# Moving the query, key and value projection of a graph layer from the sort stage to the gather stage

## The chip, the core and the metric

The kernel runs on one core of a Trainium2 chip. A core has five engines with a queue of instructions each: PE (TensorE, matrix multiplications; its weight loads are listed as PEld), DVE (VectorE), ACT (ScalarE), POOL (GpSimd) and SP (SyncE, which issues DMAs). The engines work side by side and wait for each other through semaphores; each engine takes its own instructions strictly in order. The metric is the device time of one execution in microseconds (us). Inputs are read from device memory and the result is written there within that time.

## The reference, cut to what matters

A graph layer for 6250 nodes with 256 features and 206,250 edges (src, dst). Three parts are added up: attention over the edges of the graph, linear attention over all nodes, and a mixture of eight experts.

```python
xn = layernorm(x)
# 1. graph attention: h = xn @ W (64 columns, 4 heads)
e = exp(leaky_relu(el[src] + er[dst], 0.2));  w = e / segment_sum(e, src)[src]
gnn = elu(segment_sum(w * h[dst], src) + b)            # per head, 4 x 64 = 256
# 2. linear attention, 4 heads of 32
q, k, v = split(rmsnorm(xn, g_pre) @ w_qkv)            # 128 columns each
k = softmax([mem_k, k], over the nodes);  q = softmax(q, over 32) * 32 ** -0.5
context = k @ [mem_v, v]                               # 32 x 32 a head
mix = rmsnorm((context . q) @ w_out + b_out, g_out) + xn
x = x + gnn + mix
# 3. experts: x = x + tokens + sum over the 2 best of 8 of weight * (gelu(tokens @ w1 + b1) @ w2 + b2)
```

For the linear attention every node has to contribute to `context` before any node's output can be computed, and the softmax of the keys needs a maximum over all nodes (or one that is corrected as it grows).

## The kernel before, in words

The nodes are cut into 49 tiles of 128, and `groups` are 13 runs of up to four tiles. The work goes through two stages.

**Sort stage.** The edges arrive in no order that helps. They are spread over 1612 columns of 128 and sorted into 25 pairs of node tiles by matrix products with one-hot matrices: `sort_batch` (L370 to L464) takes 32 columns at a time, in 51 batches. A batch compares on DVE (`ob`, L387), counts on PE (`n_ps`, L395), scans on DVE (`inc`, L399), ranks with two products on PE (`r_ps`, L419 and L420), takes a maximum on DVE (`rank`, L427), builds a 128 x 4096 one-hot on DVE (`ohp`, L448) and places the edges with 32 matmuls on PE (`g_ps`, L454). The loop at L526 runs `project` (L303) for a group and then three batches; the last twelve batches follow without a projection (L545). `project` loads a group of x on SP, normalizes it on ACT (`xn`, L338), transposes it on PE (`tp`, L343), and multiplies it with `wcat` (L348), a weight matrix of 456 columns: 384 for queries, keys and values, 72 for the table of the graph attention. ACT copies queries into `q_all` (L351), keys and values into `kv` (L352) and the rest into `tab` (L355), scaling the first two with `rn`, which DVE makes in small steps (L325 to L328). The table goes to device memory.

`context` (L467) is a generator: each `next` gives one step of instructions. It begins with one maximum over all keys on DVE (L468); then, step by step beside the last sort batches, POOL subtracts the maximum from the keys of a group (L498), ACT takes exponentials (L499) and PE adds keys times values to one accumulator (L502). Its last step makes the 128 x 256 matrix `cw`, which holds context and output weights.

**Gather stage.** `pack(q)` (L875) turns pair q of node tiles into gather addresses: DVE compares and scans, and seven rounds of DVE one-hots (`ohc` L923, `rc` L930, `ohp` L935) and 16 PE matmuls each (`s_ps`, L940) place the edges. Its last step issues the gathers of both tiles on POOL: 35 indirect DMAs a tile (L972) into `xe`, of which there are three buffers. So the gather of tile b + 3 can begin when tile b has been summed and its `xe` is free. For a tile, `look` (L980) makes logits (PE transposes, the ACT copy `ohT` at L1001, PE products at L1009), `weights` (L1016) turns them into edge weights on DVE and ACT, and four calls of `sums` (L1035) build weighted one-hots on DVE (`ohw`, L1041) and multiply them with the gathered rows on PE (`a_ps`, L1048). ACT's copy `a_s` (L1106) ends the tile.

Between these the loop at L1085 places other work. After each of the four `sums` of a tile it runs steps of later packs (up to `b * S + k + 3` steps of the list `packs`, eight steps a pack), and then `some_more` (L1058), which takes steps off the list `todo` until a cost is used up: in blocks of four tiles at most FC = 2 a call, 16 calls a block. `todo` begins with `attention()` (L574), 39 steps of cost 2: for each group, a softmax of the queries (L583 to L588), four transposes, products with `cw` and sums of squares (L594 to L601), and an output step that loads x again and stores `base_y` (L612 to L620). When it is used up, the expert weights are loaded (`open_experts`), and after each block the 22 steps of its experts (`finish_steps`) join the list: hidden layers (L775, L783) and results (L791, L795). Two packs, 0 and 1, are made ahead of the first tile (L1075 to L1080).

A helper `later` (L567) makes an instruction follow pack 0 in its engine's order without a wait. The order of each engine's queue is otherwise set by the framework's scheduler from the order of the program and its priorities. PSUM, in which PE writes, is divided into pools; in the gather stage `yps` has two buffers and `hps` one.

Of the kernel before, what the change touches and what calls it, by code (L numbers as in the profile page):

```python
# [1 line left out]

# [33 lines left out]
def tile_gps_layer(  # L36
# [53 lines left out]
    KW = 2 * HID + 1  # L90
    O_TAB = 3 * HID
    O_EL = O_TAB + H + FO
    PW = O_EL + H
    assert NPAD > N and PW <= 512 and last > 0
# [141 lines left out]
    with tc.tile_pool(name="ids", bufs=1) as lp:  # L236
# [21 lines left out]
    nc.scalar.dma_start(out=wcat[:, :, :3 * HID], in_=w_qkv.rearrange("(c p) f -> p c f", p=P))  # L258
    nc.scalar.dma_start(
        out=wcat[:, :, O_TAB + H:O_EL], in_=gnn_W.rearrange("(c p) f -> p c f", p=P)  # L260
    )
# [3 lines left out]
    gpre = kp.tile([P, DC], F32, name="gpre")  # L265
# [5 lines left out]
    wo = kp.tile([P, D], F32, name="wo")  # L271
    nc.scalar.dma_start(out=wo, in_=w_out)
    mk = kp.tile([P, NM], F32, name="mk")
    nc.scalar.dma_start(out=mk, in_=mem_kv[0].rearrange("h d m -> (h d) m"))
    mv = kp.tile([P, NM], F32, name="mv")
# [6 lines left out]
    for c in range(DC):  # L282
        wt_ps = mps.tile([FO, P], F32, name="tp")
        nc.tensor.transpose(wt_ps, wcat[:, c, O_TAB + H:O_EL], ident)
# [4 lines left out]
        nc.scalar.copy(wcat[:, c, O_TAB:O_TAB + H], wlr_ps[:, :H])  # L289
        nc.scalar.copy(wcat[:, c, O_EL:PW], wlr_ps[:, H:])  # L290
        nc.vector.tensor_scalar(
            wcat[:, c, :3 * HID], wcat[:, c, :3 * HID], gpre[:, c:c + 1], None, op0=OP.mult
        )

    q_all = qp.tile([P, NT, HID], F32, name="q_all")
    kv = kp.tile([P, NT, KW], F32, name="kv")
    nc.gpsimd.memset(kv[:, :, KW - 1:KW], 1.0)
    kmax = kp.tile([P, HID], F32, name="kmax")
# [4 lines left out]
    def project(t0, n):  # L303
# [10 lines left out]
        for j in range(n):  # L314
# [8 lines left out]
        rn = qw.tile([P, GT], F32, name="rn")  # L323
        nc.scalar.activation(rn[:, :n], var, AF.Sqrt, scale=float(D))
        nc.vector.tensor_mul(rn[:, :n], rn[:, :n], rs)  # L325
        nc.vector.tensor_scalar_max(rn[:, :n], rn[:, :n], 1e-12)
        nc.vector.reciprocal(rn[:, :n], rn[:, :n])
        nc.vector.tensor_scalar_mul(rn[:, :n], rn[:, :n], float(D) ** 0.5)  # L328
        shift = qw.tile([P, GT], F32, name="shift")
        nc.vector.scalar_tensor_tensor(  # L330
            shift[:, :n], stats[:, t0:t0 + n, 0], -1.0, rs, op0=OP.mult, op1=OP.mult
# [3 lines left out]
        for j in range(n):  # L335
# [3 lines left out]
                xn, xt[:, j, :], AF.Identity, bias=shift[:, j:j + 1], scale=rstd[:, t:t + 1]  # L339
# [7 lines left out]
            for c in range(DC):  # L347
# [3 lines left out]
            nc.scalar.activation(q_all[:, t, :], pr[:, :HID], AF.Copy, scale=rn[:, j:j + 1])  # L351
            nc.scalar.activation(  # L352
                kv[:, t, :2 * HID], pr[:, HID:3 * HID], AF.Copy, scale=rn[:, j:j + 1]
            )
            nc.scalar.copy(tab[:, j, :], pr[:, O_TAB:PW])  # L355
# [110 lines left out]

    def context():  # L467
        nc.vector.tensor_reduce(  # L468
            kmax, kv[:, :NT - 1, :HID].rearrange("p t d -> p d t"), axis=AX.X, op=OP.max
        )  # L470
        nc.vector.tensor_max(kmax[:last], kmax[:last], kv[:last, NT - 1, :HID])
        km_ps = mps.tile([HID, P], F32, name="tp")
        nc.tensor.transpose(km_ps, kmax, ident)
        kcol = kp.tile([P, 2], F32, name="kcol")
        nc.vector.tensor_reduce(kcol[:, 0:1], km_ps, axis=AX.X, op=OP.max)
        nc.vector.tensor_reduce(kcol[:, 1:2], mk, axis=AX.X, op=OP.max)
        kmc = kp.tile([P, 1], F32, name="kmc")
        nc.vector.tensor_max(kmc, kcol[:, 0:1], kcol[:, 1:2])
        kr_ps = mps.tile([P, HID], F32, name="tp")
        nc.tensor.transpose(kr_ps, kmc.to_broadcast([P, P]), ident)  # L480
        krow = kp.tile([P, HID], F32, name="krow")
        nc.vector.tensor_copy(krow, kr_ps)
        nkm = kp.tile([P, 1], F32, name="nkm")
# [61 lines left out]
    while batches:  # L545
        sort_batch(batches.pop(0))
        next(steps, None)
    for _ in steps:
        pass
# [714 lines left out]
```

## Time and profile before

| what | us |
|---|---|
| three runs | 4209.87, 4211.42, 4214.99; median 4211.42 |
| the profiled execution | 4182.5 |
| its span, from the first to the last instruction | 4180.7 |
| busy in the span: PE, PEld, DVE, ACT, POOL | 2268.6, 1663.9, 1919.8, 746.2, 1669.8 |
| sort stage: first matmul of the projection, last sort matmul | 25.0, 411.9 |
| first gather begins, last gather ends | 446.2, 3994.5 |
| first tile ends (`a_s`), last tile ends | 617.3, 4145.3 |
| one tile's 35 gathers, first issue to end of the last | 43.4 to 45.7 |

The profile is of one execution. Its page gives busy time by engine, the span cut into 40 slices with the busy share in tenths and the clock that PE was granted, the chain of work that ended last, and groups of instructions by line: how many, busy time in all, mean length in nanoseconds, and after the bar how long the engine had been idle before them and what ended that. Matmuls of a group overlap, so that their busy time divided by their number is less than their mean length; what follows is worked out with the former. Further views give the busy time of each engine in any stretch of time, and who waited for whom.

### The profile page before, as it was taken

Reading aid. Unit: us, or ns where it says so; the run is one execution under the profiler, and the core shown is the slowest. Engines: PE = TensorE matmul, PEld = TensorE weight load, DVE = VectorE, ACT = ScalarE, POOL = GpSimd, SP = SyncE. Lnnn points to the kernel's source line nnn. Section 1 sums busy time; section 2 is a strip of 40 time slices with the busy share of each in tenths; the row PEclk is TensorE's granted clock in tenths of the full one; section 3 lists DMA queues with packets and bytes.
Section 4 is the critical chain, followed back from the end, with each engine's and each line's share of the span. In section 5 each row is a group of like instructions: output and inputs, shape, how many; then the busy total and the mean of one; then the engine's idle time right before and its main releaser. Section 6 shows DMA issues by size and latency. Waiting matters only on the chain. (4 is left out here: it accounts for less than half of the span.)

```text
span 4180.7 us, 39357 instructions
## 1 busy us (share of the span) xinstructions
PE 2268.6 (54%) x15401; PEld 1663.9 (40%) x15401; DVE 1919.8 (46%) x3941; ACT 746.2 (18%) x1653; POOL 1669.8 (40%) x1774
## 2 busy tenths in 40 slices
PE   7877232435254764644765555455364573554677
PEld 4544232324242543433543433334253352442456
DVE  7787444536352443533442523425343452342423
ACT  5542001212111111111111110111111111110122
POOL 1001545454445344344344344544535335344410
PEclk8875555666666877776877776777676686776778
DMA  1020111111121111011011100101101001011100
GB/s 59 28 29 1 21 28 41 37 41 37 34 74 20 22 19 23 18 24 22 12 29 18 25 17 17 30 17 22 25 12 27 18 19 25 13 25 19 23 12 7
DMA packets 106548, 103.75 MB, mean 25 GB/s; under 512 B 42678, under 2 KB 78740, under 8 KB 106356
## 3 DMA queue, kind: packets, MB, share of 16 engines
q0 software_dynamic: 54720, 60.52, 8.4%
q1 hardware_dynamic: 49940, 39.75, 3.3%
q8 instruction: 123, 2.02, 0.2%
q10 hardware_dynamic: 1696, 0.89, 0.1%
q14 instruction: 69, 0.57, 0.0%
HBM read 86.39 MB, written 14.65 MB: 24 GB/s over the span
## 5 line engine op out<-in xcount | busy, mean ns | idle before, releaser
L972 POOL DMA_INDIRECT xe<-table,dst_x x1710 | 1635.7, 957 | 2011.0 <-PE a_ps L1048 1323.2
L1048 PE MATMUL a_ps<-ohw,xe 128*65 128x128 f32 x4400 | 665.1, 307 | 235.7 <-issue 189.3
L1048 PEld LDWEIGHTS a_ps<-ohw,xe 128*65 128x65 f32 x4400 | 590.8, 159 | 314.4 <-issue 243.1
L775 PE MATMUL h_ps<-tokT,w1s 128*128 128x512 f32 (+3 forms) x896 | 442.8, 610 | 235.1 <-ACT hT L783 205.1
L795 DVE SCALAR_TENSOR_TENSOR x<-y_ps,comb,x 128x256 f32<-128x256 f32 x392 | 187.0, 481 | 782.4 <-remote 479.1
L791 PE MATMUL y_ps<-w2s,hT 128*128 128x256 f32 x1568 | 436.7, 413 | 147.6 <-issue 107.2
L791 PEld LDWEIGHTS y_ps<-w2s,hT 128*128 128x128 f32 x1568 | 315.5, 208 | 273.0 <-issue 177.5
L940 PE MATMUL s_ps<-rc,ohp 128*128 128x144 f16 x2525 | 255.1, 260 | 279.5 <-DVE ohp L935 146.8
L1041 DVE TENSOR_TENSOR ohw<-oh,bank 128x1280 f32<-128x1280 bf16 x196 | 321.5, 1641 | 170.1 <-remote 149.3
L940 PEld LDWEIGHTS <-ohp 128*128 128x128 f16 x2525 | 209.6, 114 | 324.2 <-DVE ohp L935 162.9
L1009 PE MATMUL e_ps<-elw,ohT 128*128 128x48 bf16 x588 | 36.2, 199 | 544.7 <-ACT ohT L1001 477.8
L783 ACT ACTIVATE hT<-h_ps,b1s 128x512 f32<-128x512 f32 (+3 forms) x224 | 140.4, 627 | 1018.4 <-remote 531.0
L775 PEld LDWEIGHTS h_ps<-tokT,w1s 128*128 128x128 f32 x896 | 171.8, 214 | 345.7 <-ACT hT L783 226.0
L1001 ACT COPY ohT<-t_ps 128x768 bf16<-128x768 bf16 x98 | 78.3, 799 | 1130.1 <-remote 842.3
L930 DVE TENSOR_TENSOR rc<-ohc,bank 128x1152 f16<-128x1152 f16 (+1 forms) x350 | 231.2, 687 | 64.8 <-remote 62.2
L1009 PEld LDWEIGHTS <-ohT 128*128 128x128 bf16 x588 | 27.0, 106 | 577.2 <-ACT ohT L1001 505.9
L935 DVE TENSOR_TENSOR ohp<-to,bank 128x2048 f16<-128x2048 f16 (+1 forms) x175 | 193.5, 1105 | 0.0
L763 PE MATMUL y_ps<-b2s,cTs 8*128 8x256 f32 x98 | 49.7, 600 | 192.4 <-ACT cTs L761 118.6
L764 DVE TENSOR_TENSOR x<-x,y_ps 128x256 f32<-128x256 f32 x49 | 20.6, 420 | 269.7 <-remote 164.6
L1018 DVE TENSOR_REDUCE z<-e_ps 128x140 f32<-128x420 f32 (+1 forms) x49 | 28.7, 585 | 244.6 <-PE e_ps L1009 224.1
L923 DVE TENSOR_TENSOR ohc<-to,bank 128x1152 f16<-128x1152 f16 (+1 forms) x175 | 119.6, 683 | 0.3 <-ACT to L911 0.2
L448 DVE TENSOR_TENSOR ohp<-rank,iota_h 128x4096 f16<-128x4096 f16 (+1 forms) x51 | 116.1, 2277 | 6.3 <-ACT rank L439 6.0
(273 smaller groups left out, 2568.0 us busy)
## 6 DMA issues: line engine op xcount, KB each, us to landing
xe<-table,dst_x POOLq DMA_INDIRECT x1710
xt<-in_x_dram SPq DMA_DIRECT2D x24, 512.0 KB
base_y<-xt SPq DMA_DIRECT2D x12, 512.0 KB
yt<-base_y SPq DMA_DIRECT2D x9, 512.0 KB
out_dram<-x SPq DMA_DIRECT2D x9, 512.0 KB
w1s<-in_L_ffn_w_dram SPq DMA_DIRECT2D x8, 256.0 KB
w2s<-in_L_ffn_w_dram SPq DMA_DIRECT2D x8, 256.0 KB
table<-tab SPq DMA_DIRECT2D x12, 138.0 KB
```

Of the source, the lines that this page charges most:

```text
L448: nc.vector.tensor_tensor(pairs(ohp[:, :w]), two(rank2[:, :w], P // 2), row(iota_h, P // 2), op=OP.is_equal)
L775: nc.tensor.matmul(h_ps[:, :w], lhsT=w1s[:, e, c, f * P:(f + 1) * P], rhs=held["tokT"][:, c, :w], start=(c == 0), stop=(c == DC - 1),)
L783: nc.scalar.activation(held[e][:, f, :w], h_ps[:, :w], AF.Gelu, bias=b1s[:, k:k + 1])
L791: nc.tensor.matmul(y_ps, lhsT=held[e][:, f, j * P:(j + 1) * P], rhs=w2s[:, e, f, :], start=(f == 0), stop=(f == FC - 1),)
L795: results.append(nc.vector.scalar_tensor_tensor(x2[:, j, :], y_ps, held["comb"][:, j, e:e + 1], x2[:, j, :], op0=OP.mult, op1=OP.add,))
L923: nc.vector.tensor_tensor(pairs(ohc[:, :m]), twos(to[:, 0, t0:t0 + m], U * CW // 2), iota_2[:, :, :U * CW // 2].to_broadcast([P, m, U * CW ...
L930: nc.vector.tensor_tensor(pairs(rc[:, :m, i, :]), pairs(ohc[:, :m]), twos(edges_q[:, t0:t0 + m, i, :], U * CW // 2), op=OP.mult,)
L935: nc.vector.tensor_tensor(pairs(ohp[:, :m]), twos(to[:, 1, t0:t0 + m], P // 2), iota_2.to_broadcast([P, m, P // 2, 2]), op=OP.is_equal,)
L940: nc.tensor.matmul(flat(s_ps), lhsT=ohp[:, t - t0, :], rhs=flat(rc[:, t - t0]), start=(t == 0), stop=(t == NBT - 1),)
L972: nc.gpsimd.indirect_dma_start(out=xe[:, c, :], out_offset=None, in_=table, in_offset=bass.IndirectOffsetOnAxis(ap=dst_x[:, c:c + 1], axis=0),
L1041: nc.vector.tensor_tensor(ohw[:, :n], oh[:, g0:g1, i, None, :].to_broadcast([P, n, H, SN]), ew_s[:, c0:c0 + n, :, None].to_broadcast([P, n ...
L1048: nc.tensor.matmul(a_ps[:, i].rearrange("f h n -> f (h n)"), lhsT=xe[:, c, H:], rhs=ohw[:, c - c0].rearrange("p h n -> p (h n)"), start=(c ...
```

## The change

- `wcat` has 72 columns instead of 456. `project` makes only the table; it keeps `rn_all` and `shift_all`, the scales of all tiles. The buffer `kv` and the maximum over all keys are gone. The weights of queries, values and keys lie in `wqvk`, loaded by three DMAs on ACT's queue.
- `context` moves into the gather stage. It is a new generator of 41 steps: a set-up, three steps for each group and a last step. A group's first step normalizes x again (loaded again, one group ahead) and transposes it; the second makes the keys of four tiles with two matmuls of 512 columns, a running maximum on DVE, the exponentials with the factor `shrink` by which the sum so far is to be corrected, and queries and values tile by tile; the third transposes the exponentials, multiplies them with the values and adds to `sums_c`.
- `todo` begins with `context` and `attention` one after the other, 80 steps of cost 1 instead of 39 of cost 2: with 2 a call that is two steps a call.
- Packs 0, 1 and 2 are made ahead of the first tile. The list of later packs begins with pack 3, and its steps are let in eight later, so that pack 3 and those after it stand where they stood.
- `o_g` and `sq` in `attention` have one buffer instead of two.

```diff
-    O_TAB = 3 * HID
-    O_EL = O_TAB + H + FO
+    O_EL = H + FO
     PW = O_EL + H
...
+    wqvk = qp.tile([P, DC, 3, HID], F32, name="wqvk")
+    for i, k in enumerate((0, 2, 1)):
+        nc.scalar.dma_start(
+            out=wqvk[:, :, i],
+            in_=w_qkv[:, k * HID:(k + 1) * HID].rearrange("(c p) f -> p c f", p=P),
+        )
...
-            nc.scalar.activation(q_all[:, t, :], pr[:, :HID], AF.Copy, scale=rn[:, j:j + 1])
-            nc.scalar.activation(
-                kv[:, t, :2 * HID], pr[:, HID:3 * HID], AF.Copy, scale=rn[:, j:j + 1]
-            )
-            nc.scalar.copy(tab[:, j, :], pr[:, O_TAB:PW])
+            nc.scalar.copy(tab[:, j, :], pr)
...
-    steps = context()
     while batches:
         sort_batch(batches.pop(0))
-        next(steps, None)
-    for _ in steps:
-        pass
...
+    def context():
...
+        for g, (t0, n) in enumerate(groups):
+            v = vs[g % 2]
+            xnT = qw.tile([P, DC, GT * P], F32, name="xnT", bufs=1)
+            for j in range(n):
+                t = t0 + j
+                xn = xn_of()
+                nc.scalar.activation(
+                    xn, xt[:, j, :], AF.Identity, bias=shift_all[:, t:t + 1],
+                    scale=rn_all[:, t:t + 1],
+                )
+                xT_ps = yps.tile([P, DC, P], F32, name="y_ps")
+                for c in range(DC):
+                    nc.tensor.transpose(xT_ps[:, c, :], xn[:, c * P:(c + 1) * P], ident)
+                nc.scalar.copy(xnT[:, :, j * P:(j + 1) * P], xT_ps)
+            if g + 1 < len(groups):
+                xt = load(g + 1)
+            yield
+            w = (n - 1) * P + rows_of(t0 + n - 1)
+            k_ps = hps.tile([P, GT * P], F32, name="h_ps")
+            for c in range(DC):
+                nc.tensor.matmul(
+                    k_ps[:, :w], lhsT=wqvk[:, c, 2], rhs=xnT[:, c, :w],
+                    start=(c == 0), stop=(c == DC - 1),
+                )
+            here = small("here")
+            nc.vector.tensor_reduce(here, k_ps[:, :w], axis=AX.X, op=OP.max)
+            new = small("most")
+            nc.vector.tensor_max(new, most, here)
+            less = small("less")
+            nc.vector.tensor_scalar_mul(less, new, -1.0)
+            shrink = small("shrink")
+            nc.scalar.activation(shrink, most, AF.Exp, bias=less)
+            most = new
+            ekT = qw.tile([P, GT * P], F32, name="ekT", bufs=1)
+            nc.scalar.activation(ekT[:, :w], k_ps[:, :w], AF.Exp, bias=less)
+            for j in range(n):
+                qv_ps = yps.tile([P, 2, HID], F32, name="y_ps")
+                for c in range(DC):
+                    nc.tensor.matmul(
+                        flat(qv_ps), lhsT=xnT[:, c, j * P:(j + 1) * P],
+                        rhs=flat(wqvk[:, c, :2]), start=(c == 0), stop=(c == DC - 1),
+                    )
+                nc.scalar.copy(q_all[:, t0 + j, :], qv_ps[:, 0])
+                nc.scalar.copy(v[:, j, :HID], qv_ps[:, 1])
+            yield
...
+                nc.tensor.transpose(ek_ps[:r, j, :], ekT[:, j * P:j * P + r], ident)
...
+            nc.scalar.copy(ek[:r, :n], ek_ps[:r, :n])
+            c_ps = yps.tile([P, HID + 1], F32, name="y_ps")
+            for j in range(n):
+                nc.tensor.matmul(
+                    c_ps, lhsT=ek[:r, j, :], rhs=v[:r, j, :], start=(j == 0), stop=(j == n - 1)
+                )
+            nc.vector.scalar_tensor_tensor(
+                sums_c, sums_c, shrink, c_ps, op0=OP.mult, op1=OP.add
+            )
+            yield
...
-    todo = [(attention(), [FC] * (3 * len(groups)))]
+    todo = [(chain(context(), attention()), [1] * (6 * len(groups) + 2))]
...
-    for _ in pack(1):
-        pass
+    for q in (1, 2):
+        for _ in pack(q):
+            pass
 
-    packs = [steps for q in range(2, NQ) for steps in [pack(q)] * (NPB + 1)]
+    packs = [steps for q in range(3, NQ) for steps in [pack(q)] * (NPB + 1)]
...
-                while packed < min(len(packs), b * S + k + 3):
+                while packed < min(len(packs), b * S + k - 5):
```

## The prediction

> **What bounds the kernel now.** I read the page's 40 slices first, then busy time by stretches, then who waits for whom, and last the groups by line.
>
> ```profile
> PE   7877232435254764644765555455364573554677
> DVE  7787444536352443533442523425343452342423
> PEclk8875555666666877776877776777676686776778
> ```
>
> Each slice is 104.5 us. The first three (projection and sort) have both PE and DVE near 80%. From the fifth slice on (the gather stage) both are near half and nothing looks like a bound. So I took each stage apart.
>
> *Sort stage.* The first row below holds six projected groups with their 18 sort batches, the second four batches with no projection beside them.
>
> ```profile
> 111.40:242.20 130.80, 116.05 (x1368) 68.73 (x1368) 101.80 (x164) 78.84 (x306) 1.82 (x12) 0.81 0.11 32
> 373.10:400.80 27.70, 17.31 (x272) 10.82 (x272) 23.92 (x38) 3.48 (x17) 0.00 (x0) 0.50 0.00 1
> ```
>
> The columns are length, then busy PE, PEld, DVE, ACT, POOL, then the granted clock. One group takes 130.8/6 = 21.8 us with PE 19.3 and DVE 17.0. A batch alone takes 27.7/4 = 6.93 us with PE 4.33 and DVE 5.98, at a clock of 0.50 against 0.81. Three batches without any projection thus last 20.8 us, nearly as long as three with it: the wide projection fills PE, but it also stands beside the faster clock.
>
> *Gather stage.* One tile of the first ten (gather 891.5 to 935.9, next gather 959.2), cut into five stretches; then the last stretch of a later tile, which has expert work:
>
> ```profile
> 891.50:901.50 10.00, 7.09 (x59) 5.64 (x58) 6.80 (x16) 3.18 (x12) 7.66 (x8) 1.00 0.13 26
> 901.50:911.50 10.00, 0.00 (x0) 0.00 (x0) 7.62 (x19) 2.00 (x4) 7.73 (x8) 0.60 0.14 30
> 911.50:935.90 24.40, 3.36 (x31) 3.37 (x32) 2.34 (x4) 0.80 (x1) 18.61 (x20) 0.50 0.30 70
> 935.90:943.90 8.00, 4.93 (x23) 3.90 (x22) 0.00 (x0) 2.08 (x2) 0.02 (x1) 0.50 0.13 6
> 943.90:959.20 15.30, 11.81 (x76) 9.75 (x74) 13.55 (x38) 3.25 (x12) 0.00 (x0) 0.87 0.00 1
> ```
>
> ```profile
> 3120.70:3136.80 16.10, 16.10 (x133) 13.92 (x133) 14.46 (x19) 1.69 (x3) 0.00 (x0) 0.95 0.00 1
> ```
>
> While POOL gathers (44 us), PE, DVE and ACT come to a halt after some 10 to 20 us and wake when the gather has landed. The real work is done in what is left. There DVE is 89% busy in the early tile (13.55 of 15.3) and PE 100% in the later one (16.1 of 16.1). The halt shows in the waits of the late tiles as ACT waiting for something the profile cannot name:
>
> ```profile
> ACT ohT L1001 <- remote: 561.5, 21, 45.1
> ACT hT L783 <- remote: 531.0, 18, 44.3
> ```
>
> So PE's half of idle time in the gather stage is not free time. What a tile costs in two phases; counted from 0, tiles 2 to 10 end in the first row (nine) and 11 to 46 in the second (36):
>
> ```profile
> 689.00:1306.00 617.00, 251.74 (x1721) 206.30 (x1720) 303.28 (x641) 101.10 (x224) 307.27 (x315) 0.65 0.18 43
> 1306.00:4034.00 2728.00, 1496.14 (x8668) 1095.78 (x8667) 1109.51 (x2374) 389.20 (x582) 1194.80 (x1255) 0.73 0.11 21
> ```
>
> Per tile: 68.6 us with PE 28.0, DVE 33.7, ACT 11.2; then 75.8 us with PE 41.6, DVE 30.8, ACT 10.8.
>
> **The change, part by part.**
>
> ```profile
> L348 PE MATMUL pr<-wcat,xT 128*128 128x456 f32 x196 | 109.8, 690 | 5.9 <-ACT xT L345 5.9
> L791 PE MATMUL y_ps<-w2s,hT 128*128 128x256 f32 x1568 | 436.7, 413 | 147.6 <-issue 107.2
> L468 DVE TENSOR_REDUCE kmax<-kv 128x128 f32<-128x6144 f32 x1 | 11.0, 11044 | 0.0
> ```
>
> 1. *Projection, 456 columns to 72.* In the six groups L348 takes 52.3 us, 8.7 a group. The nearest narrow f32 row is L712 (8 columns, 35.6/196 = 0.18 us); 16 records of that are 2.9, so PE falls from 19.3 to 13.5. ACT loses L351 and L352 (40.7 us), DVE the four rn steps (7.9 us in 13 groups, 0.6 a group): neither led here. What is late next is DVE or the clock. Lower end: DVE alone, 17.0 - 0.6 = 16.4 us a group, a gain of 5.4 x 13 = 70 us. Upper end: three batches as in the second row, 20.8, plus 2 us where the projection's transposes and matmuls get in the batches' way, 22.8: a loss of 13 us. The cold row is the nearest, for the dense matmuls go; I take 20.6, a gain of 15 us.
>
> The granted clock is 0.81 with the wide matmuls and 0.50 without. The Trainium skill, page "TensorE: Matmul & The Clock Gate", section "Part 1: The HAM clock gate (the "warmup" mystery)", says that half clock is the default and that sustained activity lifts it; by that rule alone the stage stays at 20.8 or more, and without it 16.4 would be the better guess. The rule speaks against this change.
>
> 2. *The rest of the sort.* 16 batches lie between 286.7 and 410.9 us, with the 11.0 us reduction, the POOL subtractions (19.0 us), their exponentials and 98 context matmuls (18.1 us) among them. At 6.93 each they take 110.9: a gain of 13 us, bounds 5 and 25.
>
> 3. *Context moved into the gather stage.* In each group of four tiles: 12 transposes at 0.25 (L707, 24.9/98), 4 key records at 0.49 (L775), 16 query and value records at 0.28 (L791, 436.7/1568), 8 context records at 0.185 (L502): PE 11.0 us, 143 in all; with 0.44 for a 256-column record (L598) 176. ACT: four xn at 0.58, four copies at 0.385, eight at 0.264, exponential and copy at 0.6 each, 0.2: 7.4, so 96 us. DVE 1.4 a group and 5 for the set-up, 23 us. The order of the changed program puts 65, 68, 70, 68 and 52 of the 323 context matmuls ahead of the ends of tiles 0 to 4 and all of attention on the five tiles after; the experts open at the same tile as before, so nothing changes from tile 11 on. A context tile has PE 28.0 - 5.9 (its tenth of attention, L594 and L598, 59.1/10) + 28.6 = 50.7. That is 9 more than a late tile, whose free stretch PE fills, so 75.8 + 9 = 85, and 85 - 68.6 = 16 us more: 82 us for five. The new waits stand in ACT's and PE's queues in order: behind a key exponential that waits for PE and for DVE's maximum stand ohT, ew and a_s, the copies that release the next tile's logits and the next gather. Bounds 40 (half of it runs in the gather's first 20 us, where PE is 35% busy) and 125 (the dearer records, and ACT late).
>
> 4. *Attention at double density.* Two steps a call instead of one. DVE's attention (L583 to L619) is 120 us, 12 a tile over ten tiles, 24 over five. DVE leads there at 89%: 12 x 5 = 60, of which some runs early in the gather: 50, bounds 20 and 60. The DVE relief in the context tiles gives nothing back, since PE leads there.
>
> 5. *Third pair ahead.* The eight steps of one pack move from the first two tiles to before the first. POOL's gathers of that pair wait for buffers as before. Nothing, if they fill the halts of the first three gathers; 34 us (the first pack, 412 to 446) if they delay tile 0, whose end the fourth gather waits for. I take 0.
>
> 6. *SP and POOL queues.* 13 more loads of x (512 KB) on SP, each issued a group ahead; ACT waited for this load once, 5.1 us, in the whole run. Weights come as three DMAs instead of one and are needed 400 us later. The single buffers of o_g and sq serve steps that follow one another anyway. Nothing; at most 5.1 us a load, 66.
>
> Sum: -15 - 13 + 82 + 50 = +104 us. The profiled execution took 4182.5 us (span 4180.7): 4286.5. The median of the runs shown is 4211.42, 1.0069 times that, so I predict 4316.
>
> **Rivals.** *Faster: the sort stage falls to DVE's floor.* Gains 70 + 13, and the context fits into PE's 40 idle us a tile, so that only its 23 us of DVE shows: 4182.5 - 60 = 4122.5, as median 4151. For it: PE 89% busy in the sort stage and idle half of the gather stage. Against it: the 20.8 us of the cold batches and the halts. It decides if a group takes under 17.5 us and a context tile under 71. *No difference:* the whole 83 gained, the 82 of the context paid, attention hidden: 4211. *Slower still: handoffs.* Each group has 11 passages from PE to ACT through two y_ps buffers; ACT's wait for L594 is 48.6 us in 29 times, 1.7 each. 143 of them exposed are 243 us in place of 82: 4447.5, as median 4478. Against it: other PE work stands between.
>
> **How the numbers follow.** Forecast 0.62, faster rival 0.21, no difference 0.05, handoffs 0.12. The range leaves out the lower half of the faster rival and the upper part of the handoffs: 4165 to 4400, which takes in the bounds of parts 1 to 4 around the sum as far as they don't all fall on one side. The forecast's own range is 4240 to 4390. A measurement can tell 0.2%, 8 us, from no change. Faster 0.21, same 0.05, slower 0.74.
>
> **What will show it.** Batches of the sort stage: 20 us or more a group and a clock below 0.75 for part 1. The first gather some 28 us earlier. Tiles 0 to 4 with PE above 45 us and 80 us or more; the five after with DVE above 40; tiles from 11 on unchanged. I am wrong if the sort stage speeds up to 17 us a group, or if the halts during gathers take up the new work.

## The result, and the profile after

| | us |
|---|---|
| before, four runs | median 4210.84 (4209.87 to 4214.99) |
| after, four runs | median 4264.88 (4259.26 to 4271.08) |
| ratio | 1.0127, interval 1.0109 to 1.0144 |
| predicted | 4316 |
| profiled execution, before and after | 4182.5 and 4263.64 (spans 4180.7 and 4261.9) |

The change costs 54 us, about half of what I forecast. The profiled execution of before was 27 us quicker than any of its timed runs, so the two traces differ by 81 us where the medians differ by 54.

The slices of the page after, as those shown of before:

```profile
PE   6876243644444666465666464555355474554577
DVE  6778242535545344344353443524434343352423
PEclk9999576866666777676777676776677676776778
```

PE has less to do in the first slice and more from the sixth to the ninth. The clock row begins with 9999, and that is a trap: up to 419 us this trace has no record of the clock, and the row shows full speed for want of one. The lengths of the instructions tell the clock. Here are the placing matmuls of the sort (after the count come minimum, median and maximum in ns). First those of before in the four batches without a projection, a stretch (373.1 to 400.8 us) for which the clock is on record, at 0.50:

```profile
L454 PE MATMUL g_ps<-rv,ohp x128: 221/222/227, 373.2 to 395.3; 128*128 128x52 f16 x128
```

In the six groups of before, at a clock of 0.81, the median is 187 ns. All of before, and then all of after:

```profile
L454 PE MATMUL g_ps<-rv,ohp x1612: 184/221/253, 40.6 to 411.7; 128*128 128x52 f16 x180
```

```profile
L443 PE MATMUL g_ps<-rv,ohp x1612: 202/222/253, 37.2 to 386.0; 128*128 128x52 f16 x180
```

Before has some at 184 ns, after none below 202, and its median is that of the clock of 0.50: after the change the sort stage runs at half clock from start to end.

Two stretches of after: six groups with 18 batches, and the last 16 batches (length, then busy PE, PEld, DVE, ACT, POOL).

```profile
112.80:248.60 135.80, 113.17 (x1368) 77.65 (x1368) 100.03 (x140) 64.51 (x258) 5.78 (x12) 1.00 0.11 31
288.70:386.90 98.20, 69.06 (x1054) 43.67 (x1054) 85.91 (x124) 17.44 (x72) 1.17 (x2) 1.00 0.16 8
```

A group takes 135.8/6 = 22.6 us (21.8 before) although PE has lost 384 of its 456 columns. The same 16 batches took 124.2 us before (286.7 to 410.9) and now 98.2. The first gather begins at 420.4 instead of 446.2.

The gather stage, tiles 1 to 4, 5 to 10 and 11 to 46 (by the ends of `a_s`), first of before:

```profile
617.30:891.30 274.00, 104.48 (x746) 87.39 (x746) 129.18 (x263) 42.51 (x99) 136.57 (x140) 0.65 0.17 38
891.30:1306.30 415.00, 171.21 (x1148) 140.13 (x1147) 203.23 (x448) 68.06 (x147) 203.79 (x210) 0.65 0.18 44
1306.30:4034.70 2728.40, 1496.55 (x8669) 1096.27 (x8668) 1109.25 (x2373) 388.90 (x583) 1194.80 (x1255) 0.73 0.11 21
```

Then of after:

```profile
619.60:918.90 299.30, 159.38 (x1042) 128.34 (x1042) 122.46 (x236) 73.61 (x209) 133.44 (x140) 0.74 0.15 33
918.90:1354.10 435.20, 189.55 (x1214) 153.20 (x1211) 219.72 (x493) 77.35 (x219) 204.79 (x210) 0.66 0.22 57
1354.10:4114.70 2760.60, 1518.80 (x8688) 1104.37 (x8689) 1114.18 (x2393) 394.42 (x590) 1196.14 (x1255) 0.73 0.11 20
```

The whole difference of the traces, cut at the same events: first gather -25.8; tile 0, from the first gather to its end, 171.1 to 199.2, +28.1; tiles 1 to 4 +25.3; tiles 5 to 10 +20.2; tiles 11 to 46 +32.2; the rest +1.2. Sum +81.2. Tiles 11 to 46 have the same work in both (PE 1497 and 1519, DVE 1109 and 1114), and this line is about as large as the 27 us by which the profiled execution of before was quicker than its timed runs. Without it the sum is +49, near the 54 of the medians.

Where the new work goes is seen in one tile of after: gather from 844.6 to 888.4, next gather at 919.1.

```profile
844.60:854.60 10.00, 7.64 (x62) 5.90 (x61) 6.97 (x13) 4.84 (x11) 7.87 (x8) 1.00 0.12 25
854.60:864.60 10.00, 5.00 (x26) 2.76 (x24) 3.16 (x5) 0.00 (x0) 7.56 (x9) 0.73 0.13 28
864.60:888.40 23.80, 0.91 (x2) 0.82 (x3) 7.35 (x10) 0.43 (x2) 17.99 (x20) 0.50 0.16 33
888.40:896.40 8.00, 2.95 (x7) 1.76 (x7) 0.00 (x0) 1.54 (x6) 0.00 (x0) 0.50 0.11 6
896.40:919.10 22.70, 22.54 (x188) 20.29 (x187) 16.08 (x31) 9.36 (x26) 0.00 (x0) 0.92 0.15 48
```

The halt is there as before (PE 0.91 us of 23.8). PE now does some work in the ten us ahead of it (5.00, where the tile shown of before had 0.00), and the last stretch has become PE's: 22.54 of 22.7, where it was 11.81 of 15.3 with DVE leading.

One halt of before (PE's transposes, and the ACT copy that reads them; start, length, and in brackets how long the engine had been idle):

```profile
698.41 0.50 PE L997 MATMUL t_ps<-identb,oh 128*128 128x128 bf16 x6
738.64 0.80 ACT L1001 COPY ohT<-t_ps 128x768 bf16<-128x768 bf16 x1 [39.92 <-remote]
```

The transposes are over at 698.9, and PE does nothing from there until 739.5. ACT starts its copy 39.7 us after its input was written.

### The profile page after: what moved, and what is told of

Same layout as the page of the kernel before. It is cut to its first block, busy times and chain, and to the rows that moved or that the text cites. A ratio compares the mean times of both kernels' runs of the same rounds, so it can differ in the third digit from the quotient of the medians.

```text
span 4261.9 us, 40361 instructions
## 1 busy us (share of the span) xinstructions
PE 2354.7 (55%) x15794; PEld 1738.8 (41%) x15794; DVE 1917.0 (45%) x3946; ACT 766.3 (18%) x1763; POOL 1657.1 (39%) x1760
## 4 chain that ended last, share of the span: by engine, by line
another core or an unknown queue 27%; PE 26%; issue 7%; DVE 5%; ACT 2%; DVEq 0%; ACTq 0%
PE y_ps L842 7%; PE a_ps L1099 7%; PE h_ps L826 7%; PE s_ps L991 2%; PE y_ps L814 1%; ACT hT L834 1%; PE y_ps L763 1%; DVE ohw L1092 1%; ACT ohT L1052 1%; DVE inc L944 1%; DVE ohp L986 0%; PE t_ps L1048 0%; DVE rc L981 0%; DVE x L846 0%
## 5 line engine op out<-in xcount | busy, mean ns | idle before, releaser
L1099 PE MATMUL a_ps<-ohw,xe 128*65 128x128 f32 x4400 | 637.0, 300 | 147.8 <-issue 115.2
L1099 PEld LDWEIGHTS a_ps<-ohw,xe 128*65 128x65 f32 x4400 | 571.4, 155 | 214.6 <-issue 154.4
L842 PE MATMUL y_ps<-w2s,hT 128*128 128x256 f32 x1568 | 445.5, 418 | 143.4 <-issue 130.3
L991 PE MATMUL s_ps<-rc,ohp 128*128 128x144 f16 x2525 | 263.2, 262 | 285.9 <-issue 197.1
L991 PEld LDWEIGHTS <-ohp 128*128 128x128 f16 x2525 | 213.5, 115 | 328.7 <-issue 218.8
L815 DVE TENSOR_TENSOR x<-x,y_ps 128x256 f32<-128x256 f32 x49 | 20.6, 421 | 284.5 <-PE y_ps L814 89.0
```

What stands on the lines that cost most here:

```text
L842: nc.tensor.matmul(y_ps, lhsT=held[e][:, f, j * P:(j + 1) * P], rhs=w2s[:, e, f, :], start=(f == 0), stop=(f == FC - 1),)
L991: nc.tensor.matmul(flat(s_ps), lhsT=ohp[:, t - t0, :], rhs=flat(rc[:, t - t0]), start=(t == 0), stop=(t == NBT - 1),)
L1099: nc.tensor.matmul(a_ps[:, i].rearrange("f h n -> f (h n)"), lhsT=xe[:, c, H:], rhs=ohw[:, c - c0].rearrange("p h n -> p (h n)"), start=(c ...
```

## The experiments

I had two questions. What does each part cost, and is it really the halts that put the new work on the path? The second was answered first, unasked: most runs fell on chips (13, 11 and 9) on which **the kernel before takes 2740 to 2744 us**, not 4211. Four fell on one (15) on which it takes 4230. So each run below is compared with the kernel before on its own chip, and the runs fall into those without halts and those with.

### Both kernels again

> The kernel before, unaltered, for a second profile of it. The first four experiments ran where the kernel before took 2743 us instead of 4211; their profile shows gathers back to back, 0.3 us apart, and no halts. This run is to show the kernel before on its own side of that difference. If the halts of PE, DVE and ACT during gathers are a property of the place where a program runs and not of the program, then this profile has either the halts in all its gathers (4180 to 4215 us, tiles 11 to 46 at 75 to 77 us) or in none (2735 to 2750 us, tiles at 44 to 45 us), and first gather at 446 us in both.

> The changed kernel, unaltered, beside the kernel before on the same chip. If the halts are absent: POOL's gathers are the bound from the first gather (420.4 us) to the last, all work of the context and of attention hides beside them, and the changed kernel is faster by the 26 us by which the first gather starts earlier: 2717, ratio 0.9905, and as fast as with two pairs ahead (2720). Rival: the third pair costs or gains there by itself, so that it is 10 us or more off 2720. If the halts are present: 4265 against 4211 again, ratio 1.0127.

Both are unaltered. Before took 2744.1 in its profiled run; after 2722.06 (2721.6 to 2722.6) against 2743.58 (2741.0 to 2750.0), ratio **0.9918, interval 0.9901 to 0.9934**. On this chip the change makes the kernel faster. What is different there is in the list of waits. Of after, on the chip of the result (who waits, for whom, us in all, times, longest):

```profile
POOL xe L1023 <- PE a_ps L1099: 1423.1, 44, 50.5
ACT ohT L1052 <- remote: 715.3, 27, 45.3
POOL xe L1023 <- issue: 496.4, 1628, 0.3
```

The same kernel on chip 11:

```profile
POOL xe L1023 <- issue: 506.7, 1662, 0.3
ACT hT L834 <- PE h_ps L826: 460.4, 189, 13.7
ACT ohT L1052 <- PE t_ps L1048: 367.8, 89, 25.9
```

POOL's waits for tiles that have to be summed first are gone; 0.3 us after one gather's last DMA is issued the next is on its way. ACT's waits for something without a name ("remote", up to 45 us) are gone too: its wait for `ohT` is now one for PE. A stretch of a gather there (643.5 to 688.0):

```profile
643.50:653.50 10.00, 5.80 (x16) 3.44 (x16) 5.96 (x18) 2.10 (x9) 7.84 (x8) 0.66 0.26 30
653.50:663.50 10.00, 8.71 (x73) 7.16 (x72) 9.39 (x20) 6.66 (x18) 7.56 (x9) 1.00 0.17 27
663.50:688.00 24.50, 24.34 (x204) 21.08 (x203) 21.87 (x35) 10.43 (x31) 18.69 (x20) 1.00 0.33 77
```

PE works 24.34 us of the 24.5 in which it had 0.91 of 23.8. POOL's work in the two stretches is alike (18.69 and 17.99 us). The first line of the chain that ended last says it by engines, here of after on chip 11 and then on the chip of the result:

```profile
POOL 35%; PE 31%; DVE 13%; issue 13%; DMA 4%; ACT 3%; SPq 0%; DVEq 0%; POOLq 0%; ACTq 0%
```

```profile
another core or an unknown queue 27%; PE 26%; issue 7%; DVE 5%; ACT 2%; DVEq 0%; ACTq 0%
```

So without halts POOL's gathers are the bound from the first to the last, and the work that the change puts beside them costs nothing.

### Parts of the change, without halts

> The changed kernel with only two pairs packed ahead of the first tile, as before the change; pack 2 is spread over the first tiles again. Theory (part 5 of the prediction: the third pair ahead costs nothing, the 28 us that tile 0's stretch grew by are the context's): tile 0 takes 190 to 200 us after the first gather begins, as in the changed kernel, and the time stays at 4265, give or take 10. Rival (the third pair delays tile 0, up to the 34 us of the first pack): tile 0's stretch falls back to about 171 us and the time to 4231 to 4237, with tiles 1 and 2 paying some of it back by pack 2's steps beside them.

```diff
-    for q in (1, 2):
-        for _ in pack(q):
-            pass
+    for _ in pack(1):
+        pass
...
-    packs = [steps for q in range(3, NQ) for steps in [pack(q)] * (NPB + 1)]
+    packs = [steps for q in range(2, NQ) for steps in [pack(q)] * (NPB + 1)]
...
-                while packed < min(len(packs), b * S + k - 5):
+                while packed < min(len(packs), b * S + k + 3):
```

> The changed kernel with the context's 39 group steps left empty: x is not loaded and projected again, there are no keys, queries and values of the nodes, the queries are a constant and only the memory tokens are summed. Attention still comes two steps a call on tiles 5 to 9. The difference to the changed kernel is what the context costs in the gather stage. Theory (context costs what tiles 0 to 4 grew by, 53 us, bounds 40 and 82): 4183 to 4225, nearest 4212, with PE back near 25 us on a tile of the first five. Rival one (the context hides in the halts and the growth is the third pair's and the packs'): 4250 to 4265. Rival two (handoffs, each of the 143 passages costs): 4022 to 4150.

```diff
+    nc.gpsimd.memset(q_all, 0.5)
...
-        for g, (t0, n) in enumerate(groups):
...
+        for g in groups:
             yield
             yield
             yield
```

> As the kernel without the context's group steps (no projection of queries, keys and values of the nodes, constant queries), and attention at one step a call from tile 0 on, as before the change. Against the kernel with double density this gives the price of attention's density; against the kernel before it gives what the sort stage saved together with the third pair. Theory: the density costs 20 to 50 us, so this kernel is 20 to 50 faster than the one without context; and 26 us faster than the kernel before, 4185. Rival one (density costs nothing, since DVE's extra steps run early in the gathers): the same as the one without context, give or take 8. Rival two (the third pair costs the 28 us that the sort stage saves): 4211, the same as before.

```diff
-        for g in groups:
-            yield
-            yield
-            yield
...
-    todo = [(chain(context(), attention()), [1] * (6 * len(groups) + 2))]
+    todo = [(chain(context(), attention()), [1] * 2 + [FC] * (3 * len(groups)))]
```

The three were expected at 4185 to 4265, by the level of the result; they ran where the kernel before takes 2742.59. Two pairs: 2720.21 (ratio 0.9917). No context: 2725.55. No context, attention spread: 2725.66. The expectations in us fell with the level, but the comparison stands: two pairs ahead are as fast as three (2722.06), and taking the whole context away gains nothing. The spans less the time of the first gather make it plain: 2297 us before (2742.3 - 444.9), 2298 after (2720.2 - 421.7), 2295 with two pairs, 2295 and 2297 without context. What counts on these chips is when the first gather begins. In the two without context it begins at 430, not 421. Their first sort batch already builds its one-hot (`ohp`) 7 us later (43.5 against 36.2); ahead of it POOL fills the constant queries, 5.3 us from 16.9 us on. That this is the reason was not tested.

### Halts written into both kernels

To see whether the halts alone turn the sign, I put them into the program on a chip that has none.

```diff
+    def halt(t):
+        last_one = ready[t][0][:, columns(t) - 1, 0:1]
...
+        on_dve = nc.vector.tensor_copy(ht_d, last_one)
+        then(on_dve, halts[0])
+        halts.append(on_dve)
+        halts.append(nc.scalar.copy(ht_a, last_one))
...
                 sums(k, oh, xe, a_ps, columns(b), halts)
+                if k == 0 and b + 2 in ready:
+                    halt(b + 2)
```

`then` puts DVE's copy behind the first `ohw` of the tile, and the second `ohw` and ACT's `ohT` behind the copies, without a wait.

> The kernel before, with the halts written into the program: after the first of a tile's four sums DVE and ACT each copy one element of the last row that the gather in progress is bringing (that of the tile after next), so that the rest of the tile waits until that gather has landed. In the runs at 4211 us PE, DVE and ACT come to a halt 10 to 20 us into a gather by themselves; in the runs at 2743 us they don't. Theory (the halts are the whole difference between the two levels): a tile takes the 44 us of the gather, 3 us of landing and about three quarters of its work (25 of 33.7 us of DVE early, 31 of 41.6 us of PE late), 72 to 78 us, and the time is 3950 to 4250. Rival (the two levels differ in something else too, such as the speed of PE or of the gathers): 2750 to 3600, gathers mostly back to back.

> The changed kernel with the same halts written into the program. Theory (it is the halts that turn the change from a gain of 22 us into a loss of 54, because under them the work of context and attention stands on the path): this kernel is 20 to 90 us slower than the kernel before with written halts, its first gather 25 us earlier, its tiles 0 to 4 longer by 40 to 90 us in all, tiles 5 to 10 by 0 to 40, and the tiles from 11 on the same. Rival (the halts don't matter, the loss had another cause, a conflict of the 96 us of ACT or of the loads of x with something on that chip): 20 to 26 us faster than the kernel before with written halts.

Before with written halts 3885.73 (3883.6 to 3888.5), after 3908.13 (3904.8 to 3909.9): **+22 us, where without halts it was -22**. Tiles 1 to 4, 5 to 10 and 11 to 46 of before with written halts:

```profile
596.50:844.10 247.60, 98.78 (x758) 81.17 (x758) 131.89 (x277) 43.87 (x117) 134.80 (x140) 0.70 0.22 42
844.10:1236.70 392.60, 161.05 (x1145) 133.36 (x1145) 195.78 (x436) 63.05 (x139) 206.56 (x210) 0.66 0.22 47
1236.70:3736.80 2500.10, 1393.92 (x8659) 1073.85 (x8658) 1119.75 (x2404) 397.92 (x621) 1193.68 (x1255) 0.75 0.14 23
```

And of after:

```profile
576.40:844.50 268.10, 147.64 (x1042) 122.40 (x1042) 123.46 (x238) 74.01 (x214) 132.87 (x140) 0.77 0.20 37
844.50:1260.50 416.00, 182.69 (x1214) 148.30 (x1211) 221.17 (x501) 74.39 (x222) 202.96 (x210) 0.66 0.25 59
1260.50:3758.60 2498.10, 1392.88 (x8688) 1074.13 (x8689) 1123.88 (x2429) 406.20 (x632) 1193.78 (x1255) 0.76 0.14 23
```

First gather -25.2, tile 0 +5.1, tiles 1 to 4 +20.5, tiles 5 to 10 +23.4, tiles 11 to 46 -2.0. The pattern is the one of the result, smaller at tile 0. The written halts are milder than the real ones (before: 69.4 us a late tile instead of 75.8, and below the 3950 that I expected; tiles 0 to 4 grow by 25.6 us, below the expected 40), and the scheduler could lay work around them, so they are a model. But the halts alone turn the sign, on a chip that has none, and no other difference between the chips is needed for it. (The -22 is from chip 11, the +22 from chip 9; before takes 2744 and 2740 us on the two.)

### Parts of the change, with halts

These three carry the written halts and landed on the chip that has real ones.

> The changed kernel with written halts (3908) and the context's 39 group steps left empty: no keys, queries and values of the nodes, constant queries; attention still two steps a call on tiles 5 to 9. Under written halts the changed kernel lost 25 us on tiles 0 to 4 and 28 on tiles 5 to 11. Theory (the first part is the context's, the second attention's): 25 less on tiles 0 to 4, nothing less on 5 to 11; without the halts the first gather of this variant began 10 us later (430 against 420), which is taken back out: 3883 to 3893. Rival (the 28 us on tiles 5 to 11 are the context's as well, handed on through the queues, and density is free): 3855 to 3865. Second rival (the context is hidden, the loss of tiles 0 to 4 is the third pair's): 3908 to 3918.

> The same without the context's group steps, with written halts, and attention at one step a call from tile 0 on as before the change. Against the one before it, this is the price of attention at double density under halts. Theory (prediction's part 4, 20 to 60, DVE leads there): 20 to 28 us less than the one before it, 3855 to 3873, that is below the kernel before with written halts (3886) by about what its first gather is earlier, 15. Rival (density is free): the same as the one before it, give or take 8.

> The changed kernel with written halts and two pairs packed ahead of the first tile instead of three. Theory (part 5, the third pair costs nothing): 3900 to 3916, as with three. Rival (the third pair's 8 steps delay tile 0, by up to 34 us, and the delay stays because the gathers depend on the tiles' ends): 3874 to 3895. Opposite rival (pack 2 beside tiles 0 and 1 then stands on the path, where the context already is): 3920 to 3945.

The edits are those of the three kernels further up, on top of the written halts. Before on this chip: 4229.59. No context 4215.20 (4202.7 to 4224.0, ten runs); no context with attention spread 4182.13 (4180.2 to 4185.5); two pairs 4274.62 (4264.2 to 4276.5). The levels are again not the ones expected, since the chip halts by itself; what answers is the difference of one run from another. The changed kernel with written halts and three pairs was not run on this chip. The nearest to it is the kernel of the last experiment below: it has no written halts and differs from the changed kernel in the sort stage alone, so that its gather stage, on this chip, is that of the change. Tiles 1 to 4 and 5 to 10, without context:

```profile
611.80:856.60 244.80, 76.67 (x649) 69.43 (x648) 110.23 (x198) 17.12 (x34) 134.08 (x140) 0.64 0.15 21
856.60:1298.30 441.70, 179.84 (x1203) 143.47 (x1202) 215.85 (x478) 72.68 (x215) 205.51 (x210) 0.67 0.24 56
```

Without context, attention spread:

```profile
614.40:876.10 261.70, 108.90 (x711) 85.97 (x710) 132.32 (x267) 40.40 (x104) 138.78 (x140) 0.63 0.20 39
876.10:1283.50 407.40, 161.47 (x1139) 132.34 (x1140) 192.31 (x423) 61.40 (x145) 200.84 (x210) 0.66 0.21 45
```

With context, two pairs ahead:

```profile
608.10:923.80 315.70, 162.27 (x1079) 127.53 (x1080) 128.60 (x262) 75.15 (x217) 133.12 (x140) 0.74 0.16 32
923.80:1365.80 442.00, 191.44 (x1213) 153.66 (x1210) 221.54 (x501) 74.06 (x221) 204.96 (x210) 0.64 0.24 56
```

The changed kernel's gather stage on this chip, without written halts (kernel with fewer unused matmuls, first gather at 424.4):

```profile
625.00:925.10 300.10, 159.01 (x1041) 128.04 (x1041) 122.27 (x236) 73.59 (x208) 133.84 (x140) 0.73 0.17 33
925.10:1354.00 428.90, 189.07 (x1215) 152.76 (x1211) 219.44 (x493) 77.34 (x218) 205.50 (x210) 0.66 0.25 58
```

In one table, us, where "tile 0" is from the first gather to the end of the first tile:

| | tile 0 | tiles 1-4 | tiles 5-10 | sum |
|---|---|---|---|---|
| before (chip of the result) | 171.1 | 274.0 | 415.0 | 860.1 |
| after (chip of the result) | 199.2 | 299.3 | 435.2 | 933.7 |
| after's gather stage (this chip, no written halts) | 200.6 | 300.1 | 428.9 | 929.6 |
| two pairs | 187.3 | 315.7 | 442.0 | 945.0 |
| no context | 181.2 | 244.8 | 441.7 | 867.7 |
| no context, spread | 184.5 | 261.7 | 407.4 | 853.6 |

The last three rows are of this chip, with written halts. The two rows of after have the same work, and their sums differ by 4.1 us.

*Context:* 929.6 - 867.7 = 62 us on this chip, 933.7 - 867.7 = 66 with after on the chip of the result, and 945.0 - 867.7 = 77 with written halts on both sides but two pairs in place of three. Tiles 0 to 4 account for 72 to 77 us of it; on tiles 5 to 10 the kernels with context take the same or up to 13 us less. *Density:* tiles 5 to 10 lose 34 us, tiles 0 to 4 get 20 back, 14 net; the medians differ by 33, and about 15 of that lies in tiles 11 to 46 (2764.5 and 2749.0 us), which have the same work. I cannot say whether that is due to density. *Third pair:* up to the end of tile 4 two pairs take 503.0 us, and three 498.5 and 500.7 (both rows of after, without written halts). Nothing points to a cost; time seems to move from tiles 1 to 4 to tile 0. But the pair of runs differs in the written halts too, so this is less than shown. The spread version has 446.2 us up to tile 4, and before 445.1.

### The clock of the sort stage

> The changed kernel with eight unused matmuls of 468 columns added to each sort batch (two after the counts, two after the ranks, four after the placing), results never read: 408 more PE instructions of about 0.2 to 0.4 us each, 80 to 160 us of added PE work. Theory (the sort stage lost its gain to the half clock): the wide matmuls bring the clock back, a group falls from 22.6 us to 17 to 18.5 and a batch of the tail from 6.9 to about 6; in all 50 to 80 us less, 4185 to 4215. Rival (the batch is bound by DVE and by the handoffs between PE, ACT and DVE, and the clock matters little): groups stay at 22 or more, and the added work makes the time 4265 to 4400.

```diff
+    wm_ps = sps.tile([P, 512], F32, name="wm_ps")
+    def warm(rhs, cols, times):
+        for _ in range(times):
+            nc.tensor.matmul(wm_ps[:, :cols], lhsT=ones16, rhs=rhs, start=True, stop=True)
...
+        wc = min(18, w)
...
+        warm(flat(ob[:, :wc]), wc * NB, 2)
...
+        warm(flat(ob[:, :wc]), wc * NB, 2)
...
+        warm(rv[:, :wc // 2].rearrange("p c i b -> p (c i b)"), wc * NB, 4)
```

On a chip without halts 2687.39, ratio to before **0.9805, interval 0.9781 to 0.9829**, and below the changed kernel (2722.06) too. The first gather begins at 384.3, 36 us earlier than in the changed kernel, by adding work to PE. Three groups, and the placing matmuls:

```profile
168.00:223.50 55.50, 50.84 (x759) 33.63 (x760) 49.33 (x71) 32.37 (x130) 6.96 (x7) 1.00 0.10 28
```

```profile
L452 PE MATMUL g_ps<-rv,ohp x1612: 184/186/253, 40.3 to 349.8; 128*128 128x52 f16 x180
```

A group takes 18.5 us instead of 22.6, and the median placing matmul 186 ns instead of 222: the sort was held by the half clock. The gain of 36 us is less than the 50 to 80 that I expected.

> The changed kernel without written halts, with fewer unused matmuls of 468 columns while projections run (one, one and two a batch instead of two, two and four) and more in the last twelve batches, which have no projection (four, three and six). With twice as many PE was the bound of a group (6.6 us of 6.7 a batch at full clock, group 18.5 us). Theory (PE is released and the clock stays up): a group takes 17.0 to 17.6, near DVE's floor, the tail 6.0 a batch, the first gather begins 12 to 25 us earlier than 384, and the time falls from 2687 to 2660 to 2675. Rival (the clock needs the denser work and falls back to half in part): groups at 19 to 22.6, 2690 to 2722.

```diff
-        warm(flat(ob[:, :wc]), wc * NB, 2)
+        warm(flat(ob[:, :wc]), wc * NB, 1 if t < 3 * len(groups) else 4)
...
-        warm(flat(ob[:, :wc]), wc * NB, 2)
+        warm(flat(ob[:, :wc]), wc * NB, 1 if t < 3 * len(groups) else 3)
...
-        warm(rv[:, :wc // 2].rearrange("p c i b -> p (c i b)"), wc * NB, 4)
+        warm(rv[:, :wc // 2].rearrange("p c i b -> p (c i b)"), wc * NB, 2 if t < 3 * len(groups) else 6)
```

This one ran on the chip with halts: 4277.81 against 4229.59, ratio 1.0117 (1.0097 to 1.0138), as the changed kernel (1.0127). For the groups the rival was right; its time was meant for a chip without halts. Six groups take 134.9 us, 22.5 each, and their placing matmuls are a mixture of both lengths:

```profile
166.10:301.00 134.90, 121.59 (x1423) 76.46 (x1419) 99.65 (x142) 59.02 (x243) 6.61 (x13) 0.65 0.11 32
```

```profile
L452 PE MATMUL g_ps<-rv,ohp x576: 184/222/253, 169.7 to 294.2; 128*128 128x52 f16 x192
```

Half of the unused matmuls keep the clock up a part of the time only (0.65, against 1.00 in the three groups shown above and 0.95 from 90.3 to 229.3 us of that kernel), and no time is won; the first gather begins at 424.4. PE's busy share doesn't tell the two apart (121.59/134.9 = 0.90 and 50.84/55.5 = 0.92).

The version with more of them was not run on a chip with halts. 36 us off the changed kernel's 1.0127 would leave it at 1.004 of before there, an estimate: the gain of the sort would not pay for the context.

## Why the prediction was right in its direction and too high

The direction came out on a chip with halts, like the one whose profile I had; on a chip without them it would have been the other way. The size was too high by 50 us, and it lies in parts 3 and 4: their sum was 132 us, and tiles 0 to 10 grew by 73.6.

*Parts 1 and 2, -15 and -13.* Their sum was -28, and the first gather came 25.8 us earlier (23 on chip 11). That the sum is right is luck, for both terms were wrong. Split at the 16th batch from the end (286.7 before, 288.7 after) it is +2 and -26; the remaining -2 lie between the sort and the gather. The step that failed in part 1 is "PE falls from 19.3 to 13.5": PE has 113.17/6 = 18.9 us a group, of which the narrow projection is 27.0/6 = 4.5 where I had 2.9, and all the rest of PE's work, too, is now done at half clock. So a group takes 22.6 us, not 20.6, near the upper end that I gave (22.8) and by the mechanism named for it: without the wide matmuls the clock stays at half. The Trainium skill, page "TensorE: Matmul & The Clock Gate", section "Part 1: The HAM clock gate (the "warmup" mystery)", says that the throttled clock is the default and that activity releases it. This trace agrees with the default: placing matmuls of 222 ns throughout, against 186 with unused matmuls beside them. How much activity it takes is not read from PE's busy share: at 83% of a group (113.17/135.8) the clock stayed at half. In part 2 I took 6.93 us for each of 16 batches; they took 98.2/16 = 6.1. Most of them follow one another after 6.9 us (from one `ohp` to the next), but every fifth after 3.7; the four batches from which I had the 6.93 show only the former.

*Part 3, context, +82.* Measured 62 to 77. The mechanism was right: PE bounds the last stretch of such a tile (22.54 of 22.7 in the one shown). The step that failed is "A context tile has PE 28.0 - 5.9 + 28.6 = 50.7". Tiles 1 to 4 have PE 159.38/4 = 39.8. The 28.0 was the mean of tiles 2 to 10, and tiles 1 to 4 of before have 104.48/4 = 26.1. The context's rows came out at 132 us (L584 55.2, L566 26.3, L558 23.4, L601 17.6, L595 9.1) where I had 143, and 99 of them, 24.8 a tile where I had 28.6, fell on tiles 1 to 4; tile 0 took 29. That leaves 5 us a tile. The rows of the sums and of the packs, which I took as unchanged, went from 78.6 to 71.0 us there (L1048 and L940, after L1099 and L991), 1.9 a tile; the rest I can't assign, as rows overlap. With 39.8 in place of 50.7 my own rule, a late tile of 75.8 us with PE at 41.6, gives 74 us; tiles 1 to 4 took 74.8.

*Part 4, density, +50.* Measured on tiles 5 to 10: 20 between the two traces, 14 with after's row on chip 15, 34 between the two kernels without context, of which tiles 0 to 4 give 20 back. The step that failed is "12 a tile over ten tiles, 24 over five". Attention doesn't move as a block. Of its 13 reductions L634, the first step of the softmax, 11 ran before tile 4 ended (2 in the stretch of tile 0 and 9 in that of tiles 1 to 4), seven of them within 1 us of the last copy of their queries:

```profile
420.40:619.60 199.20, 1.36 (x2) 0.61 0.14 27
619.60:918.90 299.30, 6.08 (x9) 0.74 0.15 33
918.90:1354.10 435.20, 0.93 (x2) 0.66 0.22 57
```

(Here the first number after the length is DVE's time in L634 alone.) And the work that `attention` had before the change was already half on tiles 5 to 10. The DVE rows of attention there (before L583, L586, L588, L599, L612, L616, L619, after the same seven) went from 50.7 to 75.9 us, not by 60 but by 25, and the time by 20. The check that I named, DVE above 40 on these tiles, failed for the same reason: 219.72/6 = 36.6.

*"The DVE relief in the context tiles gives nothing back."* Between the two kernels without context, taking attention off tiles 0 to 4 gave 20 us (446.2 to 426.0). So this step failed where there is no context; with context on these tiles it can't be seen apart.

*Part 5, third pair, 0.* Right without halts (2720.21 with two pairs, 2722.06 with three); with halts nothing speaks against it, but no two runs differ in the third pair alone.

*Part 6, queues, 0.* Nothing to be seen: gathers take 43.5 to 45.7 us as before, and with all context work taken out, its loads included, the kernel gains nothing where there are no halts. With halts the loads were not tested by themselves.

*The checks.* First gather 28 us earlier: 25.8. Group at 20 us or more: 22.6. Clock below 0.75: the row can't say, the lengths say half. PE above 45 and 80 us or more on tiles 0 to 4: 39.8 and 74.8, no. Tiles from 11 on unchanged: 2728 and 2761 us of the same work, so undecided by these two traces.

*The rivals.* Handoffs would have shown in the difference between context and no context: 62 to 77 us, where 143 exposed passages came to 243. The faster rival was wrong about the sort (18.5 us a group at best, only with unused matmuls, never 16.4) and right about one thing that I had dismissed because of the halts: where they are absent the context hides in the gather stage whole.

*What was missing.* I treated the halts as a property of the program. They belong to where it ran: three of the four chips of the experiments have none, and on chip 11, where both kernels ran, the change gains 0.8%. Each chip was used once, so "chip" stands for all that differed with it. What makes some halt is not settled. The profile has no name for what ended the waits of ACT and DVE; the pair of lines above shows one that ended 39.7 us after PE had done what was waited for. On chip 11 the lists of waits of both kernels hold no nameless one. In before 62 of the 93 nameless waits of ACT and DVE above 10 us end within 10 us after the last DMA of a gather was issued, the others inside a gather.

## What to carry to other kernels

Before work is moved under a long transfer because an engine looks half idle there, find out what ends its idle time; if nothing with a name does, measure in another place before trusting either sign. Taking work off a busy PE can slow what is left, if that work kept the clock up: read the length of the same instruction before and after, not the busy share. And a block of work that is "moved" by its place in a list runs where its inputs and its engine allow: price a density from the order of each engine's queue, not from the list.

## What the runs showed of the hardware

- The same program takes 2744 us on one chip and 4211 or 4230 on another. The sort stage is equal to 2 us (first gather at 444.9 and 446.2) and a gather nearly so (43.4 to 45.7 and 43.5 to 46.1 us); what differs in the traces is the halts of PE, DVE and ACT beside POOL's indirect DMAs.
- In such a halt ACT started a copy 39.7 us after the matmuls that it waited for had ended (before, 698.9 and 738.6 us).
- Adding 408 unused matmuls to a stage in which PE was busy 83% (113.17/135.8) made it 36 us shorter; with half as many a batch beside the projection, and more behind it, it became no shorter.
- Where the profile has no record of the clock yet, its row and its stretches show full speed: 1.00 for a stage at half clock.
